# A matrix product inserted into a convolution kernel: column tiles take quarters of the outputs instead of tiles of positions, and the result is turned by a VectorE block transpose

## The chip, the cores and the metric

The kernel runs on one core of one Trainium2 chip. The metric is the device time of one execution in microseconds; the median of several runs is quoted. Every profile here shows a granted TensorE clock of 1.0 for the core. All timed runs that are compared are in the fast state; one experiment (a single look) is of unknown state, and only its trace is used.

## The reference, cut to what matters

Four layers follow each other, each with a group norm and a residual sum. Three of them are of this kind (B = 4 images of 32 x 32 positions, 16 channels):

```python
first = jnp.einsum('ijyx,byxc->bijc', Msq, inputs)      # the M product: this case
kern = ...                                              # G: a 3x3 filter set for every (i, j)
shifted = lax.conv_general_dilated(x_nchw, kern, ...)   # 1024 positions x 16 channels of outputs
diff = jax.nn.relu(inputs[:, None, None] - shifted)
second = jnp.einsum('ijyx,bijyxc->bijc', Wsq, diff)
return first - second
```

The third layer of the network is an interval layer without an M product. The convolution with its weighted sum is nearly all of the work. The M product `first` is a 1024 x 1024 matrix applied to 1024 positions x 16 channels of each image. The kernel treats the four images as two groups of two, so there are 3 layers x 2 groups = 6 M products, each with 32 columns of data (2 images x 16 channels).

## The kernel before

TensorE works through the convolution in *units*: one filter output `f` and one image `b` give ten matmul records (entries of the trace) into a pair of banks of PSUM, the memory in which matmul results are summed (`pc`); there are three pairs. VectorE reads each pair with one `scalar_tensor_tensor` that takes the minimum with 0, multiplies by the weights and sums. Everything else, the M product included, is a Python generator (`behind`) that is advanced between units; `yield 12` means "go on 12 units later".

```python
def conv_layer(phase, behind):
    ...
            for f in range(C):
                ...
                for b in range(GB):
                    ps = bank_pair(f"pc_{n}_{f}_{b}")
                    for slot in range(3):
                        for h in range(2):
                            ...
                            nc.tensor.matmul(ps[:, h, :], lhsT=w[:, f % FU, :], rhs=v[:, :, :H],
                                             start=slot == 0, stop=slot == 2)
                    ...
                    nc.vector.scalar_tensor_tensor(junk, ps.rearrange("p h n -> p (h n)"), 0.0, chunks[n],
                        op0=ALU.min, op1=ALU.mult, accum_out=acc[:, t, col : col + 1])
                    wait -= 1
                    if wait <= 0:
                        wait = next(behind, 1 << 20)
```

The M product before the change (`first_term`):

```python
xn = xns[g]                                     # normalised data, 128 positions x 8 tiles x 32 columns
fs = work.tile([P, 2, 512], F32, tag="fs", ...)
for half in range(2):                           # half of the outputs each
    mt = wpool.tile([P, NT, 512], F32, tag="MT", bufs=1, ...)
    nc.sync.dma_start(mt, convs[layer][0][half])
    yield 12
    ps = bank(f"pf_{g}{layer}{half}")
    for pt in range(NT):
        j = pt % 4
        nc.tensor.matmul(
            ps[32 * j : 32 * j + 32, :], lhsT=xn[:, pt, :], rhs=mt[:, pt, :],
            start=pt < 4, stop=pt >= 4, tile_position=(0, 32 * j),
        )
    nc.scalar.copy(fs[:, half, :], ps)
    yield 2
ps = bank(f"pfs_{g}{layer}")
for t in range(NT):
    nc.tensor.matmul(ps[:, GC * t : GC * (t + 1)],
                     lhsT=fs[:, t // 4, t % 4 * P : (t % 4 + 1) * P], rhs=stack, start=True, stop=True)
yield 2
nc.vector.tensor_tensor(X[g], X[g], ps[:, : NT * GC].rearrange("p (t m) -> p t m", t=NT), ALU.add)
```

Each of these matmuls has only 32 weight columns, and four of them run side by side on TensorE, as four column tiles `j` (in the trace of this kernel, four such records of 0.59 us start within 0.02 us). Here each column tile takes two of the eight tiles of positions, so the four results are partial sums of the same outputs. Those have to be added, and they lie the wrong way round (channels on partitions). The second set of matmuls (`pfs`) does both at once: `fs` is the stationary operand and `stack`, four identity matrices on top of each other, the moving one.

## Time and profile before

| before | |
|---|---|
| time, median | 3120.36 us at first (3 runs), 3120.57 us over 6 runs |
| TensorE matmuls busy | 3089.7 us, 99% |
| VectorE busy | 2100.3 us, 67% |
| ScalarE busy | 147.2 us, 5% |
| the M products on the path (pf and pfs) | 37.3 us, worked out in the prediction |

The page's chain answers which engine sets the end, and the timeline answers what one insertion costs. The prediction shows the lines of both and how they are read.

One more view is of use later, the waits of TensorE's matmuls (who waited for whom, microseconds in total, times, the longest):

```profile
PE pc L484 <- DMA im<-xs: 13.2, 2, 12.2
PE ps_mc L174 <- DVE part_mc L167: 8.6, 1, 8.6
PE ps_vc L174 <- DVE part_vc L167: 2.7, 1, 2.7
PE ps_t L209 <- DVE xn L195: 1.2, 1, 1.2
```

There are four kinds, each once or twice: there is no recurring wait for VectorE, although it is busy for two thirds of the time.

### The profile page before, as it was taken

The page shows a single profiled execution, that of the slowest core. Times are in us where ns is not written, and L with a number is a line of the kernel's source. Part 1 is how long each engine was busy: PE and PEld are TensorE (multiplying, and loading weights), DVE is VectorE, ACT ScalarE, POOL GpSimd, SP SyncE. Part 2 cuts the span into 40 slices and gives each one's busy share as a digit, 9 for nine tenths or more (in the row PEclk, how much of TensorE's full clock was granted, in tenths as well). Part 3 has the DMA queues.
Part 4 walks back from the last instruction along what each step waited for, and adds up shares of the span by engine and source line. Part 5 has one row for each costly group of instructions (what it writes and reads, how often), then busy time and mean ns, then how long its engine had stood idle before and what let it go on. Part 6 is the DMA issues. An engine that isn't in the chain of part 4 may idle for free.

```text
span 3119.8 us, 37923 instructions
## 1 busy us (share of the span) xinstructions
PE 3089.7 (99%) x15792; PEld 1568.0 (50%) x15792; DVE 2100.3 (67%) x3348; ACT 147.2 (5%) x159; POOL 289.2 (9%) x173
## 2 busy tenths in 40 slices
PE   6999999999999999999999999999999999999999
PEld 4444455444444444444446654444664444444444
DVE  4656666666666666666677766667776666666666
ACT  0000000000000000000000000000100000000000
POOL 2000000000000000000013300002230000000000
PEclk9999999999999999999999999999999999999999
DMA  4322111321111231211111132121113211111100
GB/s 144 123 102 75 48 68 48 125 75 66 50 62 60 69 124 48 75 48 68 48 70 52 48 118 75 48 75 48 68 48 103 97 48 70 48 72 51 67 28 2
DMA packets 32462, 215.21 MB, mean 69 GB/s; under 512 B 5665, under 2 KB 7713, under 8 KB 18465
## 3 DMA queue, kind: packets, MB, share of 16 engines
q1 hardware_dynamic: 27168, 207.02, 18.4%
q10 hardware_dynamic: 4992, 5.74, 0.9%
q8 instruction: 124, 2.03, 0.3%
q14 instruction: 50, 0.40, 0.0%
q0 software_dynamic: 128, 0.02, 0.0%
HBM read 211.64 MB, written 1.12 MB: 68 GB/s over the span
## 4 chain that ended last, share of the span: by engine, by line
PE 99%; DMA 1%; DVE 0%; ACTq 0%; issue 0%; ACT 0%
PE pc L484 97%; PE pf L255 1%; PE pfs L263 0%; DMA im<-xs 0%; PE ps_l L386 0%; DMA X<-in_x 0%; PE ps_r L397 0%; PE ps_l L384 0%; PE ps_t L209 0%; PE ps_vc L174 0%; PE ps_iv L341 0%; DMA xs<-xt 0%; PE ps_mc L174 0%; DVE xc_c L184 0%; ACTq L234 0%; DVE junk L494 0%
## 5 line engine op out<-in xcount | busy, mean ns | idle before, releaser
L484 PE MATMUL pc<-im,raw 64*128 64x512 f32 x12288 | 2920.4, 590 | 13.2 <-DMA im<-xs 13.2
L494 DVE SCALAR_TENSOR_TENSOR junk<-pc,WT 128x1024 f32<-128x1024 f32 x1536 | 1880.0, 1224 | 990.4 <-PE pc L484 986.6
L484 PEld LDWEIGHTS pc<-im,raw 64*128 64x128 f32 x12288 | 1237.2, 186 | 1137.5 <-issue 746.6
L484 PE MATMUL pc<-im,W 64*128 64x512 f32 x3072 | 1293.2, 803 | 0.0
L484 PEld LDWEIGHTS pc<-im,W 64*128 64x128 f32 x3072 | 321.1, 186 | 355.6 <-issue 343.5
L140 POOL TENSOR_TENSOR raw<-raw,pick 128x1024 f32<-128x1024 f32 x96 | 182.0, 1898 | 2278.5 <-DMA raw<-in_g 2216.9
L111 ACT ACTIVATE W<-raw,low_w 128x1024 fp32r<-128x1024 f32 x96 | 110.3, 1149 | 2198.0 <-PE pc L484 2170.1
L494 DVE DVE_READ_ACCUMULATOR junk<-pc,WT 128x1 f32 x1536 | 127.6, 83 | 0.0
L114 DVE SCALAR_TENSOR_TENSOR W<-raw,low_w,W 128x1024 fp32r<-128x1024 f32 x96 | 122.9, 1280 | 0.0
L417 POOL TENSOR_TENSOR dp_b<-ft_b,rt_r 128x1089 f32<-128x1089 f32 x16 | 39.1, 2449 | 101.6 <-ACT ft_b L410 51.5
L417 POOL TENSOR_TENSOR dp_a<-ft_a,rt_r 128x1089 f32<-128x1089 f32 x16 | 37.2, 2327 | 79.9 <-DVE s_a L424 50.2
L255 PE MATMUL pf<-MT,xn 128*32 128x512 f32 x192 | 23.1, 598 | 0.0
L424 DVE TENSOR_REDUCE s_b<-dp_b 128x33 f32<-128x1089 f32 x16 | 20.5, 1283 | 0.0
L424 DVE TENSOR_REDUCE s_a<-dp_a 128x33 f32<-128x1089 f32 x16 | 20.5, 1282 | 0.0
L114 DVE SCALAR_TENSOR_TENSOR im<-im,low_x,im 128x1088 fp32r<-128x1088 f32 x6 | 9.1, 1523 | 14.6 <-DMA im<-xs 14.6
L259 ACT COPY fs<-pf 128x512 f32<-128x512 f32 x12 | 7.0, 586 | 240.1 <-PE pf L255 240.1
L330 POOL TENSOR_SCALAR xn<-xn 128x256 f32<-128x256 f32 x2 | 1.7, 856 | 151.0 <-DVE xn L195 151.0
L506 DVE TENSOR_TENSOR X<-X,acc 128x32 f32<-128x32 f32 x48 | 13.6, 283 | 1.6
L263 PEld LDWEIGHTS pfs<-stack,fs 128*128 128x128 f32 x96 | 11.2, 191 | 3.4 <-issue 3.4
L361 DVE TENSOR_TENSOR pp<-pp 64x1024 f32<-64x1024 f32 x10 | 12.1, 1213 | 0.0
L366 DVE TENSOR_TENSOR pp<-pp 64x1024 f32<-64x1024 f32 x10 | 12.1, 1213 | 0.0
L255 PEld LDWEIGHTS pf<-MT,xn 128*32 128x32 f32 x192 | 5.0, 109 | 14.1 <-issue 14.1
(81 smaller groups left out, 160.1 us busy)
## 6 DMA issues: line engine op xcount, KB each, us to landing
raw<-in_g SPq DMA_DIRECT2D x96, 1536.0 KB, 6.6
WT<-in_w SPq DMA_DIRECT2D x48, 512.0 KB, 6.3
MT<-in_mt SPq DMA_DIRECT2D x12, 2048.0 KB, 8.3
im<-xs SPq DMA_DIRECT2D x72, 67.8 KB, 3.2
im<-xs ACTq DMA_DIRECT2D x72, 67.8 KB, 3.3
xs<-xt SPq DMA_DIRECT2D x12, 34.0 KB, 1.7
xs<-xt ACTq DMA_DIRECT2D x12, 34.0 KB, 1.8
X<-in_x ACTq DMA_DIRECT2D x2, 128.0 KB, 5.1
```

The lines of the kernel that those rows point to most:

```text
L111: nc.scalar.activation(dst, src, AF.Copy, scale=mask[:, 1:2])
L114: nc.vector.scalar_tensor_tensor(dst, src, mask[:, 0:1], dst.bitcast(F32), op0=ALU.mult, op1=ALU.add)
L140: nc.gpsimd.tensor_tensor(raw[:, 1], raw[:, 1], pick[:, f0 : f0 + FU].unsqueeze(2).to_broadcast([P, FU, P]), ALU.subtract,)
L255: nc.tensor.matmul(ps[32 * j : 32 * j + 32, :], lhsT=xn[:, pt, :], rhs=mt[:, pt, :], start=pt < 4, stop=pt >= 4, tile_position=(0, 32 * j),)
L263: nc.tensor.matmul(ps[:, GC * t : GC * (t + 1)], lhsT=fs[:, t // 4, t % 4 * P : (t % 4 + 1) * P], rhs=stack, start=True, stop=True,)
L361: nc.vector.tensor_tensor(pp[k][:, :H, M:], a[:, :H, M:], a[:, s : H + s, M:], ALU.max)
L366: nc.vector.tensor_tensor(pp[k][:, :H, M:], a[:, :H, M:], a[:, :H, M - s : M - s + H], ALU.max)
L417: nc.gpsimd.tensor_tensor(t, ft[:, i, :].unsqueeze(1).to_broadcast([P, T1, T1]), rt, ALU.add,)
L424: nc.vector.tensor_reduce(s[:, i - 1, :], last, axis=AX.X, op=ALU.max)
L484: nc.tensor.matmul(ps[:, h, :], lhsT=w[:, f % FU, :], rhs=v[:, :, :H], start=slot == 0, stop=slot == 2,)
L494: nc.vector.scalar_tensor_tensor(junk, ps.rearrange("p h n -> p (h n)"), 0.0, chunks[n], op0=ALU.min, op1=ALU.mult, accum_out=acc[:, t, co ...
L506: nc.vector.tensor_tensor(X[g][:, t], X[g][:, t], acc[:, t], ALU.add)
```

## The change

The intent is to get rid of the second set of matmuls. If each column tile takes a *quarter of the outputs* and runs over all eight tiles of positions, PSUM does the summing, and nothing is left to add (e4 and e6 below sum in this way and are correct). What remains is the turn. Output position 128 t + 32 j + i is put at column 32 t + i of column tile j, so that the turn is one of 32 x 32 blocks within partitions 32 j to 32 j + 31, and a single VectorE transpose does it (0.45 us in the trace after). The matmuls become twice as many and half as wide.

```diff
         xn = xns[g]
-        fs = work.tile([P, 2, 512], F32, tag="fs", name=f"fs_{g}{layer}")
+        ps = bank(f"pf_{g}{layer}")
         for half in range(2):
-            mt = wpool.tile([P, NT, 512], F32, tag="MT", bufs=1, name=f"MT_{g}{layer}{half}")
+            mt = wpool.tile([P, NT // 2, 4, 256], F32, tag="MT", bufs=1, name=f"MT_{g}{layer}{half}")
             nc.sync.dma_start(mt, convs[layer][0][half])
             yield 12
-            ps = bank(f"pf_{g}{layer}{half}")
-            for pt in range(NT):
-                j = pt % 4
-                nc.tensor.matmul(
-                    ps[32 * j : 32 * j + 32, :], lhsT=xn[:, pt, :], rhs=mt[:, pt, :],
-                    start=pt < 4, stop=pt >= 4, tile_position=(0, 32 * j),
-                )
-            nc.scalar.copy(fs[:, half, :], ps)
-            yield 2
-        ps = bank(f"pfs_{g}{layer}")
-        for t in range(NT):
-            nc.tensor.matmul(
-                ps[:, GC * t : GC * (t + 1)], lhsT=fs[:, t // 4, t % 4 * P : (t % 4 + 1) * P],
-                rhs=stack, start=True, stop=True,
-            )
-        yield 2
+            for k in range(NT // 2):
+                pt = NT // 2 * half + k
+                for j in range(4):
+                    nc.tensor.matmul(
+                        ps[32 * j : 32 * j + 32, :256], lhsT=xn[:, pt, :], rhs=mt[:, k, j, :],
+                        start=pt == 0, stop=pt == NT - 1, tile_position=(0, 32 * j),
+                    )
+        yield 2
+        ft = work.tile([P, NT * GC], F32, tag="fs", name=f"ft_{g}{layer}")
+        nc.vector.transpose(ft, ps[:, : NT * GC])
+        yield 1
         nc.vector.tensor_tensor(
-            X[g], X[g], ps[:, : NT * GC].rearrange("p (t m) -> p t m", t=NT), ALU.add
+            X[g], X[g], ft.rearrange("p (t m) -> p t m", t=NT), ALU.add
         )
         yield 1
```

Cut: the constant `stack` goes, and the host lays M out in the new order, with the same size of transfer. A half is now half of the contraction, not of the outputs.

More of the change, by code (lines that the diff above doesn't have):

```diff
@@ L276, in net_kernel @@
     iv = {}
-    stack = const.tile([P, GC], F32, name="stack")
     def constants():
-        nc.vector.tensor_reduce(
-            stack, ident.rearrange("p (j m) -> p m j", m=GC), axis=AX.X, op=ALU.add
-        )
         nc.scalar.dma_start(wv, iv_w)
@@ L559 @@
     for n, (pre, w) in enumerate(layers):
-        m = a[f"{pre}_M"].reshape(2, 512, NT, P)
-        give(f"mt{n}", m.transpose(0, 3, 2, 1))
+        m = a[f"{pre}_M"].reshape(NT, 4, 32, 2, NT // 2, P)
+        give(f"mt{n}", m.transpose(3, 5, 4, 1, 0, 2).reshape(2, P, NT // 2, 4, 256))
         give(f"w{n}", a[f"{pre}_{w}"].reshape(NP, NP))
```

## The prediction

> **What bounds the kernel now.** I read the page first: the busy shares, then the chain that ended last. (Columns: busy microseconds, share of the span, instructions; then the chain's shares by engine.)
>
> ```profile
> PE 3089.7 (99%) x15792; PEld 1568.0 (50%) x15792; DVE 2100.3 (67%) x3348; ACT 147.2 (5%) x159; POOL 289.2 (9%) x173
> ...
> PE 99%; DMA 1%; DVE 0%; ACTq 0%; issue 0%; ACT 0%
> ```
>
> A busy matmul row alone would prove little, since ends of matmuls are modelled, but the chain says the same: the end of the kernel is set by TensorE's order of work almost everywhere. Time taken off TensorE's queue should therefore shorten the span one for one; time taken off ScalarE or VectorE is worth nothing unless TensorE waits for it. The granted clock is 0.9 or more in all 40 slices (1.000 as a mean), so no throttle is in play.
>
> Next I read the chain in order of time around one of the six M products (start, duration, what):
>
> ```profile
> 1131.35 1.85 PE pf L255 x16
> 1133.20 27.64 PE pc L484 x137
> 1160.84 1.86 PE pf L255 x16
> 1162.70 4.12 PE pc L484 x20
> 1166.82 1.90 PE pfs L263 x16
> ```
>
> So each product stands on the path three times: two halves of pf, then the summing matmuls pfs that add the four column tiles and turn the result. Everything between is the convolution (pc). What an insertion costs is more than its own piece, so I take it from the timeline of TensorE, by the distance from the last matmul pair of one convolution unit (pc<-im,W) to that of the next: undisturbed, with a pf half between, with pfs between (start, duration, engine, line, instruction).
>
> ```profile
> 1172.04 0.80 PE L484 MATMUL pc<-im,W 64*128 64x512 f32 x2
> 1172.68 1.88 PE L484 MATMUL pc<-im,raw 64*128 64x512 f32 x8
> 1173.99 0.80 PE L484 MATMUL pc<-im,W 64*128 64x512 f32 x2
> ```
> ```profile
> 1130.54 0.81 PE L484 MATMUL pc<-im,W 64*128 64x512 f32 x2
> 1131.28 1.92 PE L255 MATMUL pf<-MT,xn 128*32 128x512 f32 x16
> 1133.13 1.99 PE L484 MATMUL pc<-im,raw 64*128 64x512 f32 x8
> 1134.56 0.81 PE L484 MATMUL pc<-im,W 64*128 64x512 f32 x2
> ```
> ```profile
> 1166.01 0.81 PE L484 MATMUL pc<-im,W 64*128 64x512 f32 x2
> 1166.75 1.97 PE L263 MATMUL pfs<-stack,fs 128*128 128x32 f32 x16
> 1168.65 1.99 PE L484 MATMUL pc<-im,raw 64*128 64x512 f32 x8
> 1170.07 0.81 PE L484 MATMUL pc<-im,W 64*128 64x512 f32 x2
> ```
>
> Undisturbed 1.96 us (1172.04 to 1173.99, rounded). With a pf half 4.02, so the half costs 2.06. With pfs 4.06, so pfs costs 2.10. Over the kernel: 12 x 2.06 + 6 x 2.10 = 24.7 + 12.6 = 37.3 us, 1.2% of the span. This is all that the change can touch on the path; the verdict can hardly leave "within 2%".
>
> [...] pf uses all 128 rows for loads and matmuls alike, yet four loads stand at 1131.74, right as a batch of four matmuls starts.
>
> ```profile
> 1131.74 0.13 PEld L255 LDWEIGHTS pf<-MT,xn 128*32 128x32 f32 x4 [0.30 <-issue]
> 1132.16 0.13 PEld L255 LDWEIGHTS pf<-MT,xn 128*32 128x32 f32 x4 [0.30 <-issue]
> ```
>
> [...] one set of four loads per batch, 0.13 us long, then nothing for 0.30 us. [...] a pf half is four batches 0.43 apart, 1.72 us, but costs 2.06; the other 0.34 us is entry and exit. [...]
>
> **The change, part by part.**
>
> Removed from the path: the whole pfs insertion, 6 x 2.10 = 12.6 us[...].
>
> Changed on the path: a half now has 16 matmuls of 256 columns instead of 8 of 512. Each fp32 matmul shows as two records, so a half goes from 16 records (four batches of four column tiles) to 32 (eight batches). Columns streamed are the same: 16 x 512 = 32 x 256. Is the batch of 256 columns really half as long? The nearest shape in the trace is ps_l, also fp32 in two records, with a new weight load for each:
>
> ```profile
> 1665.11 1.72 PE L386 MATMUL ps_l<-r,f 64*128 64x264 f32 x7
> ...
> 1666.67 0.38 PE L386 MATMUL ps_l<-r,f 64*128 64x264 f32 x1
> ```
>
> Seven steps from 1665.11 to 1666.67 are 0.223 us each at 264 columns, although each ps_l load is 0.19 us long: loads stay hidden at this length. Between 0.223 at 264 and 0.43 at 512 the slope is 0.83 ns per column, so 256 columns need 0.216 us (estimate). Four loads need 0.13 us in each 0.216, so they should hide as well, with 0.09 to spare. A half becomes 8 x 0.216 = 1.73 instead of 1.72, and with the same 0.34 at the edges 2.07. That is 12 x 0.01 = +0.1 us.
>
> Removed beside the path: 12 ScalarE copies of 0.586 us, 7 us on an engine busy for 5%; worth nothing. One small reduction for "stack" goes too.
>
> Added beside the path: 6 VectorE transposes of 128x256 from PSUM. VectorE's add of pfs, also 128x256 from PSUM, took 0.417 us; I take 0.42 for the transpose (estimate), and the add, now from SBUF, stays about 0.42. VectorE has room where they fall:
>
> ```profile
> 1174.03 0.42 DVE L268 TENSOR_TENSOR X<-X,pfs 128x256 f32<-128x256 f32 x1
> 1174.40 0.43 PEld L484 LDWEIGHTS pc<-im,raw 64*128 64x128 f32 x4 [0.24 <-DVE junk L494]
> 1174.64 1.88 PE L484 MATMUL pc<-im,raw 64*128 64x512 f32 x8
> 1174.84 1.23 DVE L494 SCALAR_TENSOR_TENSOR junk<-pc,WT 128x1024 f32<-128x1024 f32 x1 [0.39 <-PE pc L484]
> ```
>
> After the 0.42 add VectorE still idles 0.39 us; the order of the built program puts the transpose one unit ahead of the add, in a unit of its own, so each fits, with three pc bank pairs as a cushion.
>
> Moved: the second half follows the first after 12 units instead of 14. MT is loaded in between: 12 x 1.96 = 23.5 us against a slowest landing of 11.9 us, so it is still hidden.
>
> Sum: -12.6 + 0.1 = -12.5 us. 3120.4 - 12.5 = **3108 us**, 0.4% less.
>
> **Rivals.**
>
> Loads no longer hide. If each batch of 256 columns showed its 0.13 us of loads, a half would grow by 8 x 0.13 = 1.04 us, twelve halves by 12.5 us, and the gain would be gone: 3120. For it: loads per product double while each has half the time to hide behind. Against it: ps_l above hides a longer load behind nearly the same matmul.
>
> TensorE's instructions do not come fast enough. A half now has 64 PE instructions in 1.73 us, 27 ns each, against 54 ns before. At 35 ns each (an assumed figure for size) a half would take 2.24, +0.5, in all +6 us: 3114. Against it: the first 12 instructions of a pf half start within 0.05 us, so a stock of them is there; nothing in the trace shows a rate over 64. This is what the upper part of my range is for.
>
> Column tiles lose their overlap, because four matmuls now share the same xn tile. Then a half takes 32 x 0.216 = 6.9 us, +5.2 each, +62 us: 3170. Against it: before, the four tiles already ran together with four different moving streams, and the order of tiles 0, 1, 2, 3 is kept.
>
> VectorE becomes a wait: the transpose takes far longer than 0.42 us, or meets the 1.28 us weight preparation, and pc banks come free late. Even a full 0.42 us lost each time is 6 x 0.42 = 2.5 us: 3110.5. Against it: idle time of 0.73 us per plain unit, and the cushion.
>
> **Range and chances.** The 12.6 us are measured on this kernel and removed outright, so I hold them nearly sure; what is open is what the 384 shorter records cost, and it works mostly one way. I take 3105.5 to 3114.5: a little below for edges that shrink more than I count, up to half of the gain lost above. A change over 2% would need 62 us of gain, more than the 37 us at stake, or a loss of 62 us, which needs the overlap of the tiles to fail wholly: 1% each.
>
> **What the profile afterwards should show.** pfs, its loads and the ScalarE copies are gone. The pf group has 384 records of 128x256 of some 0.38 us (0.592 less 0.21), and in the chain a half still takes about 1.86 us; with batches 0.216 apart. If halves are at 2.9, loads are exposed; at 2.4, the supply of instructions; near 7, the tiles run alone. The distance from W pair to W pair over a half stays near 4.03. A transpose of about 0.42 us stands on VectorE six times, and no pc matmul waits for VectorE around it. The prediction is wrong if any of these halves is longer by over 0.5 us, or if pieces of the chain far from pf change.

## The result, and the profile after

The changed kernel takes 3108.6 us (median of 6 runs, 3105.55 to 3108.78) against 3120.57 us before (6 runs, 3119.03 to 3121.54): 12.0 us or 0.4% less. The ratio of the fast runs is 0.996, with a 95% interval of 0.9947 to 0.9973, which is "the same" at a threshold of 2% but clear of noise. All ratios here are those of the record, taken from fast runs alone; they are not quite the ratio of the medians quoted.

The profiles differ from one another before the first M product too, where the kernel starts up. The first matmul of that product starts at 125.5 us in the profile before and at 125.1 us in the one after (cut from `--tile pf`, span and matmul line of each):

```profile
core 0 of [0], span 3119.8 us
L255 PE MATMUL pf<-MT,xn x192: 592/592/617, 125.5 to 2444.1; 128*32 128x512 f32 x192
```
```profile
core 0 of [0], span 3106.9 us
L256 PE MATMUL pf<-MT,xn x384: 379/379/403, 125.1 to 2429.6; 128*32 128x256 f32 x192
```

From that matmul to the end the kernel before takes 3119.8 - 125.5 = 2994.3 us and the changed one 3106.9 - 125.1 = 2981.8 us: 12.5 us less. This *rest of the span* is used below wherever two medians are too close to be told apart. Two experiments whose code is the same up to that point, e1 and e2, reach it at 124.6 and 121.9 us, so the start alone varies by 2.7 us between profiles.

The page of the changed kernel, shares and chain:

```profile
PE 3077.5 (99%) x15888; PEld 1594.9 (51%) x15888; DVE 2102.4 (68%) x3353; ACT 140.1 (5%) x147; POOL 289.0 (9%) x173
...
PE 99%; DMA 1%; DVE 0%; ACTq 0%; issue 0%; ACT 0%
```

TensorE has 96 records more and is busy for 12.2 us less; the bound has not moved. The chain in order of time around one M product (start, duration, what):

```profile
1124.66 1.86 PE pf L256 x32
1126.52 23.72 PE pc L476 x115
1150.24 1.86 PE pf L256 x32
```

Two insertions are left of three. Each has twice the records and, at 1.86 us against 1.85 or 1.86 before, the same length. The timeline of TensorE around the first of them (here and below, the convolution's other records after the insertion are left out):

```profile
1123.85 0.81 PE L476 MATMUL pc<-im,W 64*128 64x512 f32 x2
1124.59 1.93 PE L256 MATMUL pf<-MT,xn 128*32 128x256 f32 x32
...
1127.87 0.81 PE L476 MATMUL pc<-im,W 64*128 64x512 f32 x2
```

The distance from W pair to W pair is 4.02 us (1123.85 to 1127.87), exactly what it was before with half as many, twice as wide records between. Last, all engines' timeline where the transpose falls:

```profile
1157.41 0.45 DVE L262 STREAM_TRANSPOSE ft<-pf 128x256 f32<-128x256 f32 x1
1157.77 0.44 PEld L476 LDWEIGHTS pc<-im,raw 64*128 64x128 f32 x4 [0.23 <-DVE junk L486]
1158.01 1.89 PE L476 MATMUL pc<-im,raw 64*128 64x512 f32 x8
1158.22 1.23 DVE L486 SCALAR_TENSOR_TENSOR junk<-pc,WT 128x1024 f32<-128x1024 f32 x1 [0.36 <-PE pc L476]
```

The transpose takes 0.45 us, and VectorE still idles for 0.36 us before its next convolution unit. The weight load at 1157.77 is put down to VectorE, but it starts 0.24 us ahead of its matmul, as it did before, and delays nothing. The waits of TensorE's matmuls confirm it:

```profile
PE pc L476 <- DMA im<-xs: 12.4, 2, 11.7
PE ps_mc L175 <- DVE part_mc L168: 8.7, 1, 8.7
PE ps_vc L175 <- DVE part_vc L168: 2.7, 1, 2.7
PE ps_t L210 <- DVE xn L196: 1.2, 1, 1.2
```

These are the four kinds of before, with nearly the same times and no entry for `pf` and none for a `pc` matmul behind VectorE.

### The profile page after: what moved, and what is told of

Its sections match the earlier page's. It is cut to its first block, busy times and chain, and to the rows that moved or that the text cites. A ratio compares the mean times of both kernels' runs of the same rounds, so it can differ in the third digit from the quotient of the medians.

```text
span 3106.9 us, 38106 instructions
## 1 busy us (share of the span) xinstructions
PE 3077.5 (99%) x15888; PEld 1594.9 (51%) x15888; DVE 2102.4 (68%) x3353; ACT 140.1 (5%) x147; POOL 289.0 (9%) x173
## 4 chain that ended last, share of the span: by engine, by line
PE 99%; DMA 1%; DVE 0%; ACTq 0%; issue 0%; ACT 0%
PE pc L476 97%; PE pf L256 1%; PE ps_l L378 0%; DMA im<-xs 0%; DMA X<-in_x 0%; PE ps_r L389 0%; PE ps_l L376 0%; PE ps_t L210 0%; PE ps_vc L175 0%; PE ps_iv L333 0%; DMA xs<-xt 0%; PE ps_mc L175 0%; DVE xc_c L185 0%; ACTq L235 0%; DVE junk L486 0%
## 5 line engine op out<-in xcount | busy, mean ns | idle before, releaser
L476 PEld LDWEIGHTS pc<-im,raw 64*128 64x128 f32 x12288 | 1262.1, 186 | 1108.4 <-issue 724.4
L256 PE MATMUL pf<-MT,xn 128*32 128x256 f32 x384 | 23.2, 382 | 0.0
L378 PE MATMUL ps_l<-r,f 64*128 64x264 f32 x48 | 12.1, 391 | 0.0
```

The lines of the kernel that those rows point to most:

```text
L256: nc.tensor.matmul(ps[32 * j : 32 * j + 32, :256], lhsT=xn[:, pt, :], rhs=mt[:, k, j, :], start=pt == 0, stop=pt == NT - 1, tile_position= ...
L378: nc.tensor.matmul(o, lhsT=wf[q], rhs=r[:, QI * q : QI * (q + 1), :], start=hidden is None and q == 0, stop=q == NQ - 1,)
```

## The experiments

The prediction held, so the experiments ask whether it held for its reasons. The theory is that the whole gain is the removed `pfs` insertion, and that the narrower records, the doubled weight loads and the transpose cost nothing on the path. The main rivals are that the loads are exposed and eat a part of a larger gain, that the new layout brings a part of the gain, and that VectorE has become a wait. Eight kernels were run: six against the kernel before in five rounds each, one in three, and one for a single look.

### Only the narrower records: e1_short_records

```diff
-            for pt in range(NT):
-                j = pt % 4
-                nc.tensor.matmul(
-                    ps[32 * j : 32 * j + 32, :], lhsT=xn[:, pt, :], rhs=mt[:, pt, :],
-                    ...
+            for c in range(2):
+                cs = slice(256 * c, 256 * (c + 1))
+                for pt in range(NT):
+                    j = pt % 4
+                    nc.tensor.matmul(
+                        ps[32 * j : 32 * j + 32, cs], lhsT=xn[:, pt, :], rhs=mt[:, pt, cs],
+                        ...
```

> The kernel before, with each 512-column matmul of pf cut into two of 256 columns; the column tiles still take tiles of positions, the summing matmuls and the copies stay. My theory (shorter records cost 0.01 us a half, loads hide): +0.1 us, 3120.7 us, ratio to before 1.000, W pair to W pair over a half 2.06 us above the undisturbed 1.96. Rival (loads exposed, 0.13 us a batch): +12.5 us, 3133 us, and a half at 3.1 us. Rival (the shorter records themselves are part of the gain): below 3119 us.

Measured: correct, 3120.47 us against 3120.59, ratio 0.9999 (0.9991 to 1.0008). The chain has its halves at 1.86 us, and the rest of the span is 3119.0 - 124.6 = 2994.4 us, 0.1 us longer than before. Twice as many loads in half the time each cost nothing that can be measured, and the narrower records bring nothing either.

### Only the removal of the sum: e2_no_sum

```diff
-        ps = bank(f"pfs_{g}{layer}")
-        for t in range(NT):
-            nc.tensor.matmul(ps[:, GC * t : GC * (t + 1)], lhsT=fs[...], rhs=stack, start=True, stop=True)
         yield 2
-        nc.vector.tensor_tensor(
-            X[g], X[g], ps[:, : NT * GC].rearrange("p (t m) -> p t m", t=NT), ALU.add
-        )
+        xv = X[g].rearrange("p (h t) m -> p h (t m)", h=2)
+        nc.vector.tensor_tensor(xv, xv, fs[:, :, :P], ALU.add)      # wrong on purpose
```

> The kernel before without the summing matmuls pfs; VectorE adds a part of the copied fs in their place, so the result is wrong on purpose; the ScalarE copies, the halves and their layout stay as before. My theory (the whole gain is the 2.10 us of each pfs insertion): -12.6 us, 3108 us, ratio 0.996, and the same time as the changed kernel within 1 us. Rival (a part of the gain comes from the new halves, the layout of M or the dropped copies): clearly less than the 12.0 us gained, say 3112 us or more.

Measured: wrong as intended, 3106.73 us (3105.38 to 3109.26), ratio 0.9958 (0.9944 to 0.9972). The old halves, the old layout and the ScalarE copies are all there, and the gain is still at least that of the whole change. Its median is about 2 us lower than the changed kernel's, and the interval of the ratio is about 4 us to either side, so the two cannot be told apart by time. The traces settle it: the rest of the span is 3103.7 - 121.9 = 2981.8 us, the same as the changed kernel's to 0.1 us, and the lower span of this profile comes from its start. The rival that the layout or the copies gave a part of the gain is out.

### Without the transpose: e3_no_turn

```diff
-        ft = work.tile([P, NT * GC], F32, tag="fs", name=f"ft_{g}{layer}")
-        nc.vector.transpose(ft, ps[:, : NT * GC])
         yield 1
         nc.vector.tensor_tensor(
-            X[g], X[g], ft.rearrange("p (t m) -> p t m", t=NT), ALU.add
+            X[g], X[g], ps[:, : NT * GC].rearrange("p (t m) -> p t m", t=NT), ALU.add
         )
```

> The changed kernel without the VectorE transpose: the add reads pf from PSUM directly, the result is wrong on purpose. My theory (the transpose is off the path): 3108.6 us like the changed kernel, within 0.5 us. Rival (it delays the release of pc banks): 6 x 0.44 = 2.6 us less, 3106 us.

Measured: wrong as intended, 3107.73 us (3106.7 to 3109.08), ratio 0.9958 (0.9946 to 0.9971). By its time alone this does not decide: it lies 0.9 us below the changed kernel's median and 1.7 us above the rival's figure, where the median of the kernel before moved by 0.8 us between jobs (3119.77 to 3120.59). The traces decide: in neither does a `pc` matmul wait for VectorE, and the rest of the span, which holds all six transposes, is 3106.1 - 124.3 = 2981.8 us without them and 2981.8 us with them. The transpose is off the path.

### The other order of loops: e4_tile_outer

```diff
-            for k in range(NT // 2):
-                pt = NT // 2 * half + k
-                for j in range(4):
+            for j in range(4):
+                for k in range(NT // 2):
+                    pt = NT // 2 * half + k
```

> The changed kernel with the loops of a half swapped: all four contraction steps of one column tile, then the next tile. Same instructions, same result. My theory (matmuls start in program order, so tiles overlap only where neighbours differ): a half takes 32 x 0.216 = 6.9 us instead of 1.73, less up to 3 steps where the tile changes, so +4.5 to +5.2 us for each of 12 halves: 3163 to 3171 us, ratio to before 1.014 to 1.016. Rival (TensorE reorders, or the tiles of a half overlap anyway): 3108.6 us.

Measured: correct, 3139.18 us (3138.1 to 3140.73), ratio to before 1.006 (1.0047 to 1.0073). That is 30.6 us over the changed kernel, where 54 to 62 were expected: the direction was right and the size was off by half. The timeline of TensorE shows one half:

```profile
1138.47 0.81 PE L476 MATMUL pc<-im,W 64*128 64x512 f32 x2
1139.21 4.59 PE L256 MATMUL pf<-MT,xn 128*32 128x256 f32 x32
...
1145.15 0.81 PE L476 MATMUL pc<-im,W 64*128 64x512 f32 x2
```

The distance is 6.68 us instead of 4.02, so a half costs 2.66 us more, in all 12 x 2.66 = 31.9 us. The rest of the span is 3137.5 - 123.7 = 3013.8 us, 32.0 us longer than the changed kernel's, so this accounts for it; the two whole spans differ by 30.6 us because this profile reached its first M product 1.4 us earlier. Without the edge of 0.34 us a half takes 6.68 - 1.96 - 0.34 = 4.38 us, which is 20 steps of 0.216 us with a little left over. There are 32 records, so 12 of them ran beside others, although in program order a tile's eight records (four matmuls of two records each) come before the next tile's first. Work on a tile seemed to begin four records early. My guess was a queue for each column tile; the run with marked tiles below tests the order of starts that this would give.

### The records halved once more: e5_quarter_records

```diff
-                for j in range(4):
-                    nc.tensor.matmul(
-                        ps[32 * j : 32 * j + 32, :256], lhsT=xn[:, pt, :], rhs=mt[:, k, j, :],
+                for c in range(2):
+                    for j in range(4):
+                        nc.tensor.matmul(
+                            pss[c][32 * j : 32 * j + 32, :P], lhsT=xn[:, pt, :],
+                            rhs=mt[:, k, j, P * c : P * (c + 1)],
...
-        nc.vector.transpose(ft, ps[:, : NT * GC])
+        for c in range(2):
+            nc.vector.transpose(ft[:, P * c : P * (c + 1)], pss[c][:, :P])
```

> The changed kernel with each 256-column matmul cut into two of 128 columns, in two PSUM banks, and two transposes of 128x128: same work, twice the loads. A batch of four then streams for 0.109 us, less than the 0.13 us that its four loads take. My theory (loads hide up to their own length and then set the pace): 16 batches x 0.13 = 2.1 us a half instead of 1.73, +0.35 x 12 = +4.3 us over the changed kernel, 3113 us. Rival (supply of instructions is already at its limit of 27 ns each in the changed kernel): 128 instructions x 27 ns = 3.5 us a half, +1.7 x 12 = +21 us, 3129 us. Rival (nothing is exposed): 3108.6 us.

Measured: correct, 3107.13 us (3106.47 to 3108.02), ratio 0.9959 (0.9945 to 0.9973), as the changed kernel. My theory's +4.3 us is refuted, and so is the limit on the supply of instructions. The timeline of TensorE:

```profile
1122.97 0.81 PE L479 MATMUL pc<-im,W 64*128 64x512 f32 x2
1123.71 1.95 PE L257 MATMUL pf<-MT,xn 128*32 128x128 f32 x64
...
1127.01 0.81 PE L479 MATMUL pc<-im,W 64*128 64x512 f32 x2
```

The distance is 4.04 us for 64 records. I had added the start offsets of the four loads (6.6 ns from one to the next) to the length of one (0.11 us), 0.13 us in all, and taken that as time in which TensorE is occupied. It is not: a batch of four takes (4.04 - 1.96 - 0.34) / 16 = 0.109 us. (The rest of the span is 3106.1 - 124.1 = 2982.0 us, 0.2 us longer than the changed kernel's.)

### Records of 64 columns: e8_64_columns

To find where loads do show, the kernel *before* (each piece is a closed accumulation group, and with pieces of 256 columns, in e1, the result was correct) got pieces of 64 columns:

```diff
-            for pt in range(NT):
-                j = pt % 4
+            for c in range(8):
+                cs = slice(64 * c, 64 * (c + 1))
+                for pt in range(NT):
+                    j = pt % 4
                     ... ps[32 * j : 32 * j + 32, cs], lhsT=xn[:, pt, :], rhs=mt[:, pt, cs], ...
```

> The kernel before (halves, copies and sum as there) with each 512-column matmul of pf cut into eight of 64 columns. A batch of four would stream for 0.055 us, half the 0.11 us that one load record lasts. Theory A (a load occupies its column tile for as long as its record, and sets the pace): 32 batches x 0.11 = 3.5 us a half instead of 1.72, +1.8 x 12 = +21 us, 3142 us. Theory B (most of the 0.11 us is latency, and loads still hide): +0.1 us a half at most, 3122 us or less. Theory C (supply of instructions at 6.6 ns each: 8 in a batch need 0.053 us, just enough): as B. A value between, near 0.08 us a batch, would mean that a load occupies its tile for part of its record.

Measured: correct, 3121.47 us (3119.64 to 3122.55) against 3119.77, ratio 1.0004 (0.9995 to 1.0013). The timeline of TensorE:

```profile
1130.17 0.81 PE L486 MATMUL pc<-im,W 64*128 64x512 f32 x2
1130.91 1.99 PE L257 MATMUL pf<-MT,xn 128*32 128x64 f32 x128
...
1134.25 0.81 PE L486 MATMUL pc<-im,W 64*128 64x512 f32 x2
```

The distance is 4.08 us, so 128 records with 128 loads cost 0.06 us more than 16 with 16. A batch of four takes (4.08 - 1.96 - 0.34) / 32 = 0.056 us, half as long as the record of one of its loads (0.11 us), with loads and matmuls both on all 128 rows. Each batch has one load for each tile, so at least half of a load's record here is not time in which its tile is kept from the next load. At which width the loads begin to show was not reached.

### Which record is whose: e7_marked_tiles

```diff
             for j in range(4):
+                w = 224 if j % 2 else 256
                 for k in range(NT // 2):
                     ...
-                        ps[32 * j : 32 * j + 32, :256], lhsT=xn[:, pt, :], rhs=mt[:, k, j, :],
+                        ps[32 * j : 32 * j + 32, :w], lhsT=xn[:, pt, :], rhs=mt[:, k, j, :w],
```

> e4 (tile outer) again, with column tiles 1 and 3 cut to 224 columns so that their records can be told from those of tiles 0 and 2 (256 columns); the last 32 columns are dropped from the result, so it is wrong on purpose. e4 cost half of what strict program order would: 20 steps of 0.216 us for the 32 records of a half. Theory A (each column tile has a queue of its own, some four records deep, so a later tile starts before an earlier one has started all of its records): the first 224-column record starts within 0.02 us of the fifth 256-column record, and three 256-column records of tile 0 start after it. Theory B (matmuls start strictly in program order, and the 20 steps come from something else): no 224-column record starts before eight 256-column records have started.

Measured: wrong as intended, one run of 3136.21 us (state unknown). In the trace of the half that starts at 1138.15 us (starts to the nanosecond are read from the packed trace, since `prof` prints two decimals), the first four matmul records start alone, at 1138.153, 1138.393, 1138.609 and 1138.825, all of 256 columns. The fifth of 256 columns starts at 1139.041, the first of 224 columns at 1139.046, and three more of 256 columns follow at 1139.256, 1139.472 and 1139.688. The same is seen at the next change: tile 1's fifth record starts at 1139.827 and tile 2's first at 1139.833. The answer on this line of the kernel for the stretch from 1139.035 to 1139.8 us, which also takes in the record begun at 1138.825, counts them (duration in ns, then forms):

```profile
L257 PE MATMUL pf<-MT,xn x9: 352/379/379, 1138.8 to 1139.7; 128*32 128x256 f32 x5, 128*32 128x224 f32 x4
```

The starts are those that theory A expected, to the record, and theory B is out: matmuls of different column tiles do not start in program order here. The first 224-column record starts 5 ns after the fifth of 256 columns, and the last of the three that follow starts 0.64 us after it. The queue itself, and what sets the number four, these runs do not show. The number gives e4's total: each change of tile overlaps four of eight records, 32 - 3 x 4 = 20 steps.

### Both halves in one insertion: e6_one_insertion

```diff
+        mts = []
         for half in range(2):
-            mt = wpool.tile([P, NT // 2, 4, 256], F32, tag="MT", bufs=1, ...)
-            nc.sync.dma_start(mt, convs[layer][0][half])
+            mts.append(wpool.tile([P, NT // 2, 4, 256], F32, tag="MT", bufs=2, ...))
+            nc.sync.dma_start(mts[half], convs[layer][0][half])
             yield 12
+        for half in range(2):
+            mt = mts[half]
             for k in range(NT // 2):
```

> The changed kernel with two MT buffers, so that both halves run back to back at the place of the second: one insertion for each product instead of two. My theory (entry and exit of the column tiles cost 0.34 us for each insertion): 6 x 0.34 = 2.0 us less than the changed kernel, 3106.5 us. Rival (the edge goes with the amount of work, or the first batch of the second half waits): 3108.6 us.

Measured: correct, 3105.47 us (3105.15 to 3106.81), ratio to before 0.9955 (0.9942 to 0.9967). The timeline of TensorE:

```profile
1145.85 0.81 PE L479 MATMUL pc<-im,W 64*128 64x512 f32 x2
1146.59 3.66 PE L259 MATMUL pf<-MT,xn 128*32 128x256 f32 x64
...
1151.60 0.81 PE L479 MATMUL pc<-im,W 64*128 64x512 f32 x2
```

The distance of 5.75 us makes 3.79 us for the whole product, against 2 x 2.06 = 4.12. So a saved insertion is worth 0.33 us, 2.0 us in all: the edge goes with the number of insertions, as predicted. This version beats both kernels in its trace and has the lowest median; in the same job it leads e5, which takes the changed kernel's time, by 1.7 us. Since the start varies by as much, the trace carries this verdict more than the time does. Its first M product comes 12 units (23.5 us) later; from there to the end it takes 3104.4 - 148.1 = 2956.3 us, against 2981.8 - 23.5 = 2958.3 us for the changed kernel: 2.0 us less.

## Why the prediction was right

- **TensorE's queue sets the end, one for one.** Right. The 12.5 us worked out came back as 12.0 us in the medians, 12.9 us in the two profiled spans (3119.8 and 3106.9) and 12.5 us in the rest of the span, from the first M product on. The other 0.4 us of the spans lies in the start, where the longest wait for `im` was 12.2 us before and 11.7 us after. By the letter this is the prediction's last sign of being wrong, a piece of the chain far from pf that changed; but the start varies by more than that between runs of the same code (e1 and e2), so it says nothing against the account.
- **The removed insertion is the gain.** Right: e2 takes it away alone and has the whole gain, and e1 changes the halves alone and has none.
- **A half of narrower records costs the same.** Right in its result (2.06 us each, as before; to the nanosecond the packed trace has a mean W-to-W distance of 4.014 us before and 4.020 after, +0.006 us a half where 0.01 was worked out), and the length of a record, some 0.38 us, is as said: the page has 382 ns as the mean of 384. The reason given for hidden loads was too timid. I counted 0.13 us of load in each 0.216 us, with 0.09 to spare. e5 and e8 show that loads stay hidden with batches down to 0.056 us. The rival of exposed loads and that of a short supply of instructions were therefore both further away than the range allowed for; e8 gets 256 TensorE instructions through in 1.92 us, 7.5 ns each.
- **The transpose is beside the path.** Right: 0.446 us against 0.42 estimated, the add 0.42 us, and no wait of a matmul behind it. The 224 columns of e7 took 0.411 us, so a column more costs some 1.1 ns. The accumulation left open over both halves also gives a right result (e4, e5 and e6 have the same start and stop flags and are correct).
- **The later half still finds M loaded.** Right: no `pf` matmul waits for a transfer in the list of waits; M's slowest landing was 12.0 us, in a gap of 23.7 us.
- **Losing the overlap of tiles.** This rival did not occur. When e4 provoked a part of it, my figure for it (strict program order, some 5 us a half) was twice what came, because a tile's first four records start beside the last four of the tile before (in e7 the first of them 5 ns after that tile's fifth).

## What to carry to other kernels

When one engine's queue sets the end, cost an inserted piece by the distance between two like instructions around it, not by its own record: here that gave 2.10 us for a piece of 1.90 us, and it forecast the gain to within a microsecond. Partial sums that lie in different column tiles have to be added by somebody (here by pfs, 2.10 us for each product); if the tiles split the outputs instead of the contraction, PSUM adds at no extra time (a half cost 2.06 us before and after), and a turn in 32 x 32 blocks can go to an engine with room (here VectorE, 0.446 us off the path). Let the column tile be the innermost loop (the other order cost 31 us here), and gather insertions of column-tile matmuls into one (e6 saved 0.33 us for each).
